# A vision state-space block and a resampled MLP on one core: first loads, filter order, upsampling buffers and downsampling loads rearranged

## The chip, the core and the metric

The program runs on one core of one Trainium2 chip. The core has five instruction streams that run side by side and meet at semaphores: TensorE (PE: matrix products, PEld is its loading of weights), VectorE (DVE), ScalarE (ACT), GpSimd (POOL), and SyncE (SP), which here only issues DMA transfers. Each engine takes its instructions in order, so one that waits holds back everything behind it on its engine. The metric is the device time of one execution in microseconds (us). All data is float32.

## The reference

Eight images of 64 x 64 pixels with 96 channels pass two residual layers. The first is a selective scan over the pixels in four directions (rows and columns, forward and backward); the second is a pointwise quadratic network between an upsampling by two and a low-pass downsampling. Cut to what matters:

```python
# layer 0:  x = x + ss2d(group_norm(x))
xc, z = split(x @ in_proj.T)                       # 192 channels each
xa = silu(depthwise_conv3x3(xc) + conv_b)
xs = stack([xa by rows, xa by columns, both reversed])   # K = 4
dts, B, C = split(x_proj[k] @ xs)
delta = softplus(dt_proj[k] @ dts + dt_b);  A = -exp(A_logs)
h[t] = exp(delta[t] * A) * h[t-1] + delta[t] * xs[t] * B[t]   # 16 states a channel, 4096 steps
y = sum over the four directions of (C . h + D * xs), each turned back
out = (layer_norm(y) * silu(z)) @ out_proj.T
# layer 1:  x = x + mlp(group_norm(x))
h = upsample2_by_fft(x) @ W1.T + b1
h = coef0 + coef1 * h + coef2 * h * h
out = lowpass_by_fft(h @ W2.T + b2)[::2, ::2]
```

## The kernel before

**The scan is the backbone.** An image has 4 directions, 4 chunks of 1024 pixels in each, and 24 tiles in a chunk: a tile is 8 channels x 16 states on 128 partitions and 1024 steps on the free axis. That makes 384 tiles an image and 3072 in all, in the order of the list `tiles`; the direction order is k = 1, 0, 2, 3. For a tile, SP fetches `du` spread over the states (`dub`, L1020), GpSimd multiplies it by B (`bb`, L1026), TensorE spreads delta into PSUM (`pd`, L1032), ScalarE takes its exponential in place (L1039), VectorE runs the recurrence (L1046), and VectorE or, for every third tile, GpSimd multiplies by C (`hc`, L1052). TensorE sums over the states (`py`, L1084), ScalarE copies the sum out (L1117). `hold` keeps the last state for the next chunk (`carry`, L1065). The loop over `i` at the end issues, for each tile, the fetch six tiles ahead, `bb` three ahead and `pd` one ahead.

**All other work is threaded between the tiles.** The order of instructions is written out by hand. Work items are Python generators; each `yield` ends a piece and names what the next piece costs (`pe`, `act`, `dve`, `dma`, and `bank`, one of three PSUM banks). `Side.advance` is called once per tile and issues pieces: first `stores`, then `hurried` (which takes from `urgent`), then `active` (which takes from `queue`), within the budgets of `CAPS`. An item has a greatest number of items that may be active beside it, and a weight; new items start only while the weight begun is below what is due at that tile, and at most two per call. `Side.drain` does the same without budgets until nothing is left; it is used before the loop and after it.

**The items of an image.** `front` loads an image's pixels (`piece`, L500), transposes them into `pad` (L429, copies L433), takes statistics (L435), normalizes (`norm`, L513), and runs twelve filter units (`conv`, L524: nine taps; the filter is the projection times the tap, `w_tap`) and twelve gate units (`gate`, L590). Filter units for the second 64 channels cover two blocks of 512 pixels at once. Results go to DRAM (`u_dram`, L556), and `lay` stores the row order. `prepare` makes a chunk's operands: `begin` loads `u` (L933), `project` makes B and C (`px`, L944, then `br` and `cr`), `delta` makes delta (`pv`, L969) and `du` in thirds (L988, L991). `tail` adds the directions, normalizes, gates and adds the residual into `x1` (L646 to L719). `mlp` upsamples the columns (`up_h`, L768, L769, stored to DRAM by L775), then handles five rows at a time (`rows_`, L804 to L849), then downsamples (`down_h`, load L864, transposes L872, products L878, L882, L892) and stores the image. While image b is scanned, the side work is the `tail` and `mlp` of image b - 1 and the `front` of image b + 1. For the last image `tail` starts in its last direction, and `mlp` is drained after the last scan.

**Before the loop.** The constants come in over SP and ScalarE in turn (`queue`, L154 and following) and are worked up in one block (L218 to L350), on PSUM tiles of their own. Then `front(0)` is drained with its first eight filter units, then the first chunk's `prepare`; then six fetches, and the loop. The second chunk's `begin` is made urgent before the loop, the rest of its `prepare` at i = 0.

**Buffers that matter here.** `up_h` copies two halves of 512 columns into one tile `t1s` of a pair of buffers. `down_h` loads `t3r` into one of two buffers, lets one step pass and then takes a bank; at most two units are between load and end.

Of the kernel before, what the change touches and what calls it, by code (L numbers as in the profile page):

```python
# [8 lines left out]
F32 = mybir.dt.float32  # L9
AF = mybir.ActivationFunctionType  # L10
# [126 lines left out]
def kernel(ctx: ExitStack, tc: tile.TileContext, a: dict, out: bass.AP):  # L137
# [19 lines left out]
    ident = load("ident", [128, 128])  # L157
    grp = load("grp", [C, C])
# [11 lines left out]
    nc.vector.tensor_scalar(cen_w[:, 1, :], mean_w, -1.0, None, ALU.mult)  # L170
    nc.vector.tensor_tensor(cen_w[:, 0, :], ident[:C, :C], mean_w, ALU.subtract)
# [21 lines left out]
    nc.scalar.activation(neg_a, neg_a, AF.Exp)  # L193
    nc.vector.tensor_scalar(neg_a, neg_a, -1.0, None, ALU.mult)
# [22 lines left out]


    pieces = [(0, 0, 64, 0, 0), (1, 0, 32, 0, 64), (1, 32, 64, 1, 0), (2, 0, 64, 1, 32)]
    with tc.tile_pool(name="ps0", bufs=1, space=PSUM) as ps0, tc.tile_pool(name="setup", bufs=1) as c0p:  # L220
        w_cin = load("w_cin", [C, DI], c0p)

        w_tap = convr
        for tap in range(9):
            nc.vector.tensor_tensor(w_tap[:, tap, :], convr[:, tap, :], w_cin, ALU.mult)
        sel_0 = c0p.tile([128, 8, 128], F32, name="sel_0")
        for hf in range(2):
            queue().dma_start(
                sel_0[64 * hf : 64 * hf + 64].rearrange("p j m -> p (j m)"),
                a["sel_b"][0:64, 0:2].rearrange("r q j m -> r (q j m)"),  # L230
            )
        nc.vector.tensor_copy(sel_b, sel_0.rearrange("p j (c n) -> p j n c", n=NS))
        xp_in = [
            c0p.tile([128, K, Q3, R if n == "xp_dt" else NS], F32, name=n) for n in ("xp_dt", "xp_c", "xp_b")
        ]
        d_sum = c0p.tile([128, Q3], F32, name="d_sum")
        ds = c0p.tile([128, Q3, K], F32, name="ds")
        for hf in range(2):
            for q, r0, r1, f, c0 in pieces:
                rows, src = slice(64 * hf + r0, 64 * hf + r1), slice(c0, c0 + r1 - r0)  # L240
                for t, name in zip(xp_in, ("xp_dt", "xp_c", "xp_b")):
                    queue().dma_start(t[rows, :, q, :], a[name][src, :, f, 0 : t.shape[-1]])
                queue().dma_start(ds[rows, q, :], a["ds"][src, f, :])
        nc.gpsimd.memset(xp, 0.0)
        for t, c0 in zip(xp_in, (0, 32, 48)):
            nc.vector.tensor_copy(xp[:, :, :, c0 : c0 + t.shape[-1]], t)
        nc.vector.tensor_reduce(d_sum, ds, mybir.AxisListType.X, ALU.add)
        for q in range(Q3):
            nc.vector.tensor_scalar(d_diag[:, q, :], ident, d_sum[:, q : q + 1], None, ALU.mult)

        ramp = c0p.tile([128, 128], F32, name="ramp")
        ones = c0p.tile([128, 128], F32, name="ones")
        nc.gpsimd.memset(ones, 1.0)
        nc.vector.tensor_tensor_scan(ramp, ones, ones, -1.0, ALU.mult, ALU.add)
        nc.vector.tensor_tensor(ones, ident, ramp, ALU.mult)
        freq = c0p.tile([128, 1], F32, name="freq")
        nc.vector.tensor_reduce(freq, ones, mybir.AxisListType.X, ALU.add)
        NF = 33
        wave = c0p.tile([NF, 2 * (SIDE + 64)], F32, name="wave")
        turn, half, poly = (c0p.tile(wave.shape, F32, name=f"wave{j}") for j in range(3))  # L260
        cols, c0 = {}, 0
        for quarter in range(2):
            for n in (SIDE, 64):
                at = cols[n, quarter] = slice(c0, c0 + n)
                c0 += n
                m, r = wave[:, at], turn[:, at]
                nc.vector.tensor_scalar(m, ramp[:NF, :n], freq[:NF], -quarter * n / 4.0, ALU.mult, ALU.add)

                nc.vector.tensor_scalar(r, m, 1.0 / n, 12582912.0, ALU.mult, ALU.add)
                nc.vector.tensor_scalar(r, r, -12582912.0, -float(n), ALU.add, ALU.mult)  # L270
                nc.vector.tensor_tensor(r, m, r, ALU.add)
                nc.vector.tensor_scalar(half[:, at], r, math.pi / n, None, ALU.mult)
        nc.vector.tensor_tensor(turn, half, half, ALU.mult)
        nc.vector.tensor_scalar(poly, turn, 1.0 / math.factorial(13), -1.0 / math.factorial(11), ALU.mult, ALU.add)
        nc.vector.tensor_tensor(poly, poly, turn, ALU.mult)
        for j in (9, 7, 5, 3):
            c = (1.0 if j % 4 == 1 else -1.0) / math.factorial(j)
            nc.vector.scalar_tensor_tensor(poly, poly, c, turn, ALU.add, ALU.mult)
        nc.vector.scalar_tensor_tensor(poly, poly, 1.0, half, ALU.add, ALU.mult)
        nc.vector.tensor_tensor(poly, poly, poly, ALU.mult)  # L280
        nc.vector.tensor_scalar(wave, poly, -2.0, 1.0, ALU.mult, ALU.add)

        share = c0p.tile([NF, 2], F32, name="share")
        for j, n in enumerate((64, SIDE)):
            nc.vector.tensor_scalar(share[:, j : j + 1], ident[:NF, 0:1], -1.0 / n, 2.0 / n, ALU.mult, ALU.add)
        nc.vector.scalar_tensor_tensor(
            share[:, 1:2], ident[:NF, 32:33], -1.0 / SIDE, share[:, 1:2], ALU.mult, ALU.add
        )
        down_f = c0p.tile([NF, 2, 64], F32, name="down_f")
        up_f = c0p.tile([NF, 2, 2, 64], F32, name="up_f")  # L290
        for quarter in range(2):
            base = wave[:, cols[64, quarter]]
            nc.vector.tensor_scalar(down_f[:, quarter, :], base, share[:, 1:2], None, ALU.mult)
            for j in range(2):
                nc.vector.tensor_scalar(up_f[:, quarter, j, :], base, share[:, 0:1], None, ALU.mult)
        pf = ps0.tile([128, SIDE + 64], F32, name="pf")
        for quarter in range(2):
            grid = wave[:, cols[SIDE, quarter]]
            start, stop = quarter == 0, quarter == 1
            nc.tensor.matmul(  # L300
                pf[:, :SIDE],
                up_f[:, quarter].rearrange("p a j -> p (a j)"),
                grid,
                start=start,
                stop=stop,
                skip_group_check=True,
            )
        for quarter in range(2):
            grid = wave[:, cols[SIDE, quarter]]
            start, stop = quarter == 0, quarter == 1  # L310
            nc.tensor.matmul(
                pf[:SIDE, SIDE:], grid, down_f[:, quarter, :], start=start, stop=stop, skip_group_check=True
            )
# [986 lines left out]
```

## Time and profile before

| | us |
|---|---|
| median of three runs | 11214.56 (11200.23 to 11256.48) |
| the profiled execution | 11227.57 |
| its span, first to last instruction | 11225.8 |
| first filter matmul | 42.97 |
| first scan | 142.55 |
| last scan begins | 10928.46 |

In the profile's lists a row of a timeline has the start, the duration, the engine, the line of the kernel, the operation, the tiles (out<-in), the shapes, the count, and in brackets the idle time of the engine before it and what ended that. A row of the waits has who waited for whom, the total in us, the number of times and the longest. Slices are forty equal parts of the span, each digit the busy tenths. "issue" means that the profile shows nothing that the engine waited for.

### The profile page before, as it was taken

The numbers are of one execution on the slowest core, as the hardware profiler recorded it, in microseconds if no ns is written. First come the engines' busy times: TensorE is split into PE (matmuls) and PEld (weight loads), VectorE is DVE, ScalarE is ACT, GpSimd is POOL, SyncE is SP. The second block draws the span as 40 slices with busy tenths as digits, with TensorE's granted clock in tenths as the row PEclk, the third lists the DMA queues.
The fourth block names the chain that finished last, engine by engine and source line by source line (L and its number), as shares of the span: only waits on it lengthen the run. The fifth ranks groups of instructions, "written<-read, shape, count | busy, mean of one in ns | idle before, by whom it ended". The sixth has DMA issues, their size and how long they took to land. (4 is left out here: it accounts for less than half of the span.)

```text
span 11225.8 us, 137177 instructions
## 1 busy us (share of the span) xinstructions
PE 10052.8 (90%) x45022; PEld 3217.9 (29%) x45022; DVE 10212.6 (91%) x7711; ACT 5906.0 (53%) x8218; POOL 10175.5 (91%) x4665
## 2 busy tenths in 40 slices
PE   7898888999889998899889998899988999889888
PEld 2222222322223222332223322233222332223224
DVE  5999999999999999999999999999999999999980
ACT  4455444656455564555545555455644656455443
POOL 4999999999999999999999999999999999999990
PEclk9999999999999999999999999999999999999998
DMA  5878898899988999888988989889898899988981
GB/s 145 220 201 224 211 232 206 215 225 234 230 206 217 230 231 226 209 221 222 236 213 215 222 215 246 206 216 225 221 240 207 216 225 232 231 208 215 224 198 41
DMA packets 1045102, 2401.26 MB, mean 214 GB/s; under 512 B 293948, under 2 KB 315708, under 8 KB 1044392
## 3 DMA queue, kind: packets, MB, share of 16 engines
q1 hardware_dynamic: 1040872, 2391.03, 85.8%
q8 instruction: 361, 5.91, 0.2%
q14 instruction: 349, 2.86, 0.1%
q10 hardware_dynamic: 3520, 1.46, 0.1%
HBM read 1929.05 MB, written 328.73 MB: 201 GB/s over the span
## 5 line engine op out<-in xcount | busy, mean ns | idle before, releaser
L1026 POOL TENSOR_TENSOR bb<-dub,br 128x1024 f32<-128x1024 f32 x3072 | 7174.5, 2359 | 254.7 <-DMA dub<-du 167.9
L1039 ACT ACTIVATE pd<-pd,neg_a 128x1024 f32<-128x1024 f32 x3072 | 3340.3, 1087 | 4592.7 <-PE pd L1032 4566.6
L1032 PE MATMUL pd<-dl,sel_b 64*128 64x512 f32 x12288 | 3528.3, 647 | 942.1 <-DVE carry L1065 625.6
L1046 DVE TENSOR_TENSOR_SCAN pd<-pd,carry,bb 128x1024 f32<-128x1024 f32 x1536 | 3610.1, 2350 | 287.7 <-ACT carry L1065 117.5
L1052 POOL TENSOR_TENSOR hc<-h,cr 128x1024 f32<-128x1024 f32 x1024 | 2413.9, 2357 | 370.8 <-DVE h L1046 303.1
L1052 DVE TENSOR_TENSOR hc<-pd,cr 128x1024 f32<-128x1024 f32 x2048 | 2508.1, 1225 | 157.2 <-PE py L1084 14.7
L1032 PEld LDWEIGHTS pd<-dl,sel_b 64*128 64x128 f32 x12288 | 967.7, 186 | 3230.9 <-issue 1534.8
L1046 DVE TENSOR_TENSOR_SCAN h<-pd,carry,bb 128x1024 f32<-128x1024 f32 x768 | 1796.2, 2339 | 7.8 <-ACT pd L1039 7.4
L1084 PE MATMUL py<-hc,sel_r 128*32 128x512 f32 x12288 | 1723.2, 620 | 34.6 <-POOL hc L1052 34.4
L1046 DVE TENSOR_TENSOR_SCAN pd<-pd,bb 128x1024 f32<-128x1024 f32 x512 | 1173.1, 2291 | 149.5 <-ACT pd L1039 68.7
L1058 PE MATMUL idle<-sel_b,ident 128*128 128x512 f32 x1654 | 949.4, 656 | 5.2 <-DVE ty L682 5.2
L524 PE MATMUL pc<-pad,convr 96*128 96x512 f32 (+1 forms) x2304 | 858.7, 614 | 2.0 <-issue 2.0
L1046 DVE TENSOR_TENSOR_SCAN h<-pd,bb 128x1024 f32<-128x1024 f32 x256 | 583.3, 2278 | 26.1 <-ACT pd L1039 24.3
L988 POOL TENSOR_TENSOR u<-dl,u 128x512 f32<-128x512 f32 x384 | 486.0, 1272 | 126.9 <-DMA br<-xd 126.7
L1084 PEld LDWEIGHTS py<-hc,sel_r 128*32 128x32 f32 x12288 | 251.1, 109 | 1115.3 <-issue 862.0
L821 PEld LDWEIGHTS p<-w2q,mq 128*100 128x100 f32 x4800 | 452.6, 168 | 274.5 <-issue 214.4
L814 PE MATMUL ph<-xu,w 96*128 96x500 f32 x960 | 505.7, 630 | 11.5 <-ACT mq L815 6.7
L821 PE MATMUL p<-w2q,mq 128*100 128x96 f32 x4800 | 511.1, 258 | 2.3 <-ACT mq L815 2.3
L944 PE MATMUL px<-u,xp 64*64 64x512 f32 x1536 | 427.4, 630 | 37.4 <-DMA u<-u 35.0
L1058 PEld LDWEIGHTS idle<-sel_b,ident 128*128 128x128 f32 x1654 | 252.9, 191 | 613.5 <-issue 575.5
L524 PEld LDWEIGHTS pc<-pad,convr 96*128 96x128 f32 (+1 forms) x2304 | 262.2, 162 | 561.5 <-issue 559.3
L969 PE MATMUL pv<-xd,dt_w 64*64 64x512 f32 x1536 | 398.5, 610 | 2.0 <-ACT xd L954 2.0
(153 smaller groups left out, 6763.1 us busy)
## 6 DMA issues: line engine op xcount, KB each, us to landing
dub<-du SPq DMA_DIRECT2D x3072, 512.0 KB
u<-u SPq DMA_DIRECT2D x256, 384.0 KB
du<-u SPq DMA_DIRECT2D x768, 128.0 KB
y<-yq SPq DMA_DIRECT2D x768, 128.0 KB
br<-xd SPq DMA_DIRECT2D x256, 256.0 KB
cr<-xd SPq DMA_DIRECT2D x256, 256.0 KB
yp<-y SPq DMA_DIRECT2D x384, 128.0 KB
yp<-u SPq DMA_DIRECT2D x192, 128.0 KB
```

The lines of the kernel that those rows point to most:

```text
L524: nc.tensor.matmul(t[rows].rearrange("p (i j) -> p i j", i=8), weights[:, cs], v["pad"][:, 8 * blk + kw : 8 * blk + kw + 8, kh : kh + H], ...
L814: nc.tensor.matmul(t[:, :px], w1[:, m, :], xu, start=True, stop=True)
L821: nc.tensor.matmul(t[:SIDE, C * i : C * i + C], sq[:, m, row], w2q[:, m, :], start=(m == 0), stop=(m == 2))
L944: nc.tensor.matmul(p[rows], xp[rows, k, q, :], v["u"][rows, q, :], start=(q == 0), stop=(q == 2), skip_group_check=True,)
L988: nc.gpsimd.tensor_tensor(v["u"][:, q, :], got["dl"][:, q, :], v["u"][:, q, :], ALU.mult)
L1026: nc.gpsimd.tensor_tensor(t["bb"], t["dub"], t["got"]["br"], ALU.mult)
L1032: nc.tensor.matmul(pd[:, MB * hf : MB * hf + MB], sel_b[rows, 4 * t["s"] + t["j"]].rearrange("p n c -> p (n c)"), t["got"]["dl"][rows, t[" ...
L1039: nc.scalar.activation(pd, pd, AF.Exp, scale=neg_a[:, t["k"], t["g"] : t["g"] + 1])
L1046: nc.vector.tensor_tensor_scan(t["h"][:, ::step], pd[:, ::step], t["bb"][:, ::step], 0.0 if t["first"] else held, ALU.mult, ALU.add)
L1052: (nc.gpsimd if t["by_pool"] else nc.vector).tensor_tensor(t["hc"], t["h"], t["got"]["cr"], ALU.mult)
L1058: nc.tensor.matmul(p, ident, sel_b[:, 0:4].rearrange("p j n c -> p (j n c)"), start=True, stop=True)
L1084: nc.tensor.matmul(py[r0 : r0 + 32], sel_r[:, t["j"], :], t["hc"][:, MB * hf : MB * hf + MB], start=(t["j"] == 0), stop=(t["j"] == 3 and t ...
```

## The change

1. `x1`, the buffer for an image's pixels that `tail` used to take from a pool, becomes a constant tile, and image 0 is loaded into it right behind the first constant, by eight loads on SP. The statistics of image 0 read it in place of loads of their own.
2. The products for `w_tap` move from VectorE to GpSimd. The other small constants are loaded behind the pixels, all over SP (`constants_in`), and are worked up by two items, `constants_of_scans` and `constants_of_mlp`, that are drained together with the first filter units; they take their PSUM from the three side banks.
3. Only four filter units are drained ahead of the first chunk's `prepare`. The next four are the queue while it is issued, with doubled budgets. The second chunk's `begin` is made urgent at i = 2, the rest at i = 4.
4. `up_h` copies each half into a tile of its own, in a ring of five.
5. `down_h` lets four steps pass between the load and the bank. For the last image eight units may be between load and end, with eight buffers in a pool of their own.

```diff
     ident = load("ident", [128, 128])
+    x1 = cp.tile([128, 32, C], F32, name="x1")
+    for w in range(0, 32, 8):
+        for wh in range(2):
+            w0 = 32 * wh + w
+            nc.sync.dma_start(x1[64 * wh : 64 * wh + 64, w : w + 8, :], x[0, :, w0 : w0 + 8, :])
     grp = load("grp", [C, C])
...
+    w_cin = load("w_cin", [C, DI])
+    w_tap = convr
+    for tap in range(9):
+        nc.gpsimd.tensor_tensor(w_tap[:, tap, :], convr[:, tap, :], w_cin, ALU.mult)
...
+    def constants_in():
+        nc.gpsimd.memset(xp, 0.0)
+        raw["sel"] = tile_([128, 8, 128], "sel_0")
...
+                    nc.sync.dma_start(t[rows, :, q, :], a[name][src, :, f, 0 : t.shape[-1]])
+                nc.sync.dma_start(ds[rows, q, :], a["ds"][src, f, :])
...
+    def constants_of_scans():
+        yield {}
+        nc.scalar.activation(neg_a, neg_a, AF.Exp)
+        nc.vector.tensor_scalar(neg_a, neg_a, -1.0, None, ALU.mult)
+        nc.vector.tensor_copy(sel_b, raw["sel"].rearrange("p j (c n) -> p j n c", n=NS))
+        yield dict(bank=1)
+        bank, pt = side.bank("pt")
...
+    def constants_of_mlp():
+        yield {}
+        nc.vector.tensor_scalar(cen_w[:, 1, :], mean_w, -1.0, None, ALU.mult)
...
         def piece(g):
+            if b == 0:
+                return x1[:, 4 * g : 4 * g + 4, :]
             yield dict(dma=200)
...
         if b == 0:
-            return start + convs[:8], convs[8:] + lays + gates + [bp.close()]
+            return start + convs[:4], convs[4:] + lays + gates + [bp.close(), bp.close()]
...
-            keep["x1"] = bp.tile([128, 32, C], F32, tag="x", name="x", bufs=1, depth=0)
+            keep["x1"] = x1
...
+        deep = 8 if b == images - 1 else 2
...
         def up_h(j):
-            s = bp.tile([SIDE, 2, MB], F32, tag="t1s", name="t1s")
+            s = []
...
-                nc.scalar.copy(s[:, wh, :], t[:SIDE])
+                s.append(bp.tile([SIDE, MB], F32, tag="t1s", name="t1s", bufs=5))
+                nc.scalar.copy(s[wh], t[:SIDE])
...
-            while v["rows"] < SIDE // 10 or v.get("down", 0) >= 2:
+            while v["rows"] < SIDE // 10 or v.get("down", 0) >= deep:
                 yield {}
             v["down"] = v.get("down", 0) + 1
-            s = bp.tile([SIDE, 2, 4 * C], F32, tag="t3r", name="t3r", bufs=2, depth=1)
+            s = bp.tile([SIDE, 2, 4 * C], F32, tag="t3r", name="t3r", bufs=deep, depth=1 if deep == 2 else 2)
...
-            yield {}
+            for _ in range(4):
+                yield {}
             yield dict(bank=1, pe=0.95, act=0.8)
...
-            + [bp.close()],
-            [(4, 2, lambda j=j: down_h(j)) for j in range(8)],
-            [bp.close(), bp.close()],
+            + [bp.close()]
+            + [bp.open("deep")] * (deep > 2),
+            [(max(4, deep), 2, lambda j=j: down_h(j)) for j in range(8)],
+            [bp.close()] * (2 + (deep > 2)),
...
-        side.queue, rest = front(0)
+        side.queue = [bp.open("setup")]
+        side.drain()
+        constants_in()
+        start, rest = front(0)
+        side.queue = start[:-4]
+        side.drain()
+        side.queue = start[-4:] + [(8, 0, constants_of_scans), (8, 0, constants_of_mlp)]
         side.drain()
         side.urgent = prepare(0, tiles[0]["k"], tiles[0]["i0"], tiles[0]["got"])
-        side.drain()
+        side.queue, rest = rest[:4], rest[4:]
+        while side.urgent or side.hurried:
+            side.advance({e: (2 * most, 2 * most) for e, (_, most) in Side.CAPS.items()}, 2, 0)
...
-        side.urgent.append(begin)
         total = 1
...
-            if i % NT == 0:
+            if i == 2:
+                side.urgent.append(begin)
+            if i == 4 or i and i % NT == 0:
                 side.urgent += side.later
                 side.later = []
```

## The prediction

> **What bounds the kernel now.** I read the page's busy times and slices first. They say that VectorE and GpSimd are full from slice 1 to slice 38, so a gain has to come from the two ends, or from places inside where both stop.
>
> ```profile
> span 11225.8 us, 137177 instructions
> PE 10052.8 (90%) x45022; PEld 3217.9 (29%) x45022; DVE 10212.6 (91%) x7711; ACT 5906.0 (53%) x8218; POOL 10175.5 (91%) x4665
> DVE  5999999999999999999999999999999999999980
> POOL 4999999999999999999999999999999999999990
> ```
>
> Then the timeline of the first 200 us. The eight filter units take TensorE 64.63 us before any scan. The first scan starts at 142.55, 35 us after they end. The second chunk's projection (L944) is put into TensorE's queue at once and waits there for `u`; all that is behind it waits too, and VectorE loses 14.96 us. The thirteenth scan (tile 12) starts at 199.68.
>
> ```profile
> 42.97 64.63 PE L524 MATMUL pc<-pad,convr 96*128 96x512 f32 x216 [2.00 <-issue]
> 142.55 2.30 DVE L1046 TENSOR_TENSOR_SCAN pd<-pd,bb 128x1024 f32<-128x1024 f32 x1 [10.39 <-POOL bb L1026]
> 155.72 3.75 PE L944 MATMUL px<-u,xp 64*64 64x512 f32 x4 [24.26 <-DMA u<-u]
> 164.66 2.29 DVE L1046 TENSOR_TENSOR_SCAN h<-pd,bb 128x1024 f32<-128x1024 f32 x1 [14.96 <-ACT pd L1039]
> 199.68 2.30 DVE L1046 TENSOR_TENSOR_SCAN pd<-pd,bb 128x1024 f32<-128x1024 f32 x1 [0.31 <-ACT carry L1065]
> ```
>
> Third, the waits inside the loop (200 to 10920 us), and one upsampling and one downsampling stage in the timeline. ScalarE's copy into `t1s` waits for the store that frees its buffer; the exponential behind it is late, and the scan with it. At the end of a downsampling stage TensorE waits for `t3r`.
>
> ```profile
> ACT t1s L769 <- DMA t<-t1s: 88.9, 21, 9.2
> ...
> 3249.08 0.58 ACT L769 COPY t1s<-p 100x512 f32<-100x512 f32 x1 [8.46 <-DMA t<-t1s]
> 3250.75 2.30 DVE L1046 TENSOR_TENSOR_SCAN pd<-pd,bb 128x1024 f32<-128x1024 f32 x1 [7.26 <-ACT pd L1039]
> ...
> 2405.19 1.01 PE L878 MATMUL p<-t3r,down_t 100*64 100x384 f32 x4 [2.29 <-DMA t3r<-t]
> 2413.33 2.36 DVE L1046 TENSOR_TENSOR_SCAN pd<-pd,carry,bb 128x1024 f32<-128x1024 f32 x1 [2.05 <-ACT pd L1039]
> ```
>
> Last, the end: eight downsampling units, one every 6.61 us, each with a wait for `xn`, at half clock (the columns are stretch, TensorE busy, granted clock, DMA share, GB/s).
>
> ```profile
> 11181.05 1.55 PE L878 MATMUL p<-t3r,down_t 100*64 100x384 f32 x4 [0.92 <-ACT xn L874]
> 11187.67 1.55 PE L878 MATMUL p<-t3r,down_t 100*64 100x384 f32 x4 [0.93 <-ACT xn L874]
> ...
> 43.00:47.00 4.00, 4.00 (x5) 0.50 0.02 4
> 47.00:60.00 13.00, 13.00 (x31) 0.99 0.00 0
> 11160.00:11226.00 66.00, 45.01 (x144) 0.53 0.24 65
> ```
>
> **The change, part by part.** The sum is made against the profiled execution (11227.57 us, span 11225.8), which lies 13.0 us above the median of the three runs (11214.56); the difference is then taken off the median.
>
> *Start of the filters (now 42.97).* The pixel loads leave SP's queue at 0.7 instead of 22.7: eight issues of about 0.63 us (twelve took 7.55). They are 1.5 MB; at the 200 GB/s that the loop moves that is 8 us, so they land by about 11. Passed by them on SP: `grp`, two of the `conv_b` loads and six more, 5 us later each. VectorE's queue has the add into `low` (L185) ahead of the statistics; it waits for `conv_b`, at 9.2 now, 12.5 then. Eight statistics steps follow, each a chain transpose 0.61, copies 0.64, statistics 0.69 in two banks: 1.15 each (1.3 now, beside loads), so they end near 21.5. Reduction to `nb` takes 3.2 (38.84 to 42.05) and the first matmul follows 0.9 later: 25.5. Beside it GpSimd makes the nine filters: its 512 and 1024 wide products take 1.27 and 2.36 us, so 192 wide 0.59, nine 5.3; `w_cin` lands near 14, the border memsets follow, 21. Covered, by 4 us; without that cover it delays one for one. All small constants now go over SP, 38 issues at about 0.62, until some 36: covered, since the first store of a filter unit comes at 47 (64.22 now, 21 after the filters' start); were they later, that store would wait 0.62 for each. Bounds for the filters' start: 22 (loads free of each other) and 36 (the copies into `pad` held back by the late border memsets).
>
> The Trainium skill, GPSIMD Engine Reference, § 3.1, speaks against this move: an elementwise product of two tensors costs GpSimd about twice VectorE's time. The rows agree (2.36 against 1.22 for the same product), and by either the nine are off the path.
>
> *Four units ahead of chunk 0.* Now the first four units take 42.97 to 76.4, 33.4; with the new start they end at 58.9. The constants' VectorE chain (13 us of short operations) lies beside units three and four. From the end of the units to `u` in place: 10.7 to 12.4 now (118.35 and 119.96 against 107.6), plus two issues for `dt_w`, 1.5: 72.8. Then TensorE's order decides: all of units five to eight are issued ahead of the first `pd`. 36 filter steps at 0.86 are 31.0; the projection and three `pv` steps, 6 x 0.86, 5.2; `pd` 1.1; the exponential 1.1; 1.7 for the slow clock at the restart: first scan near 113. The data side is ready earlier: last `pv` at 95, its ScalarE, VectorE and GpSimd steps to 100.5, store, load 4.6 and product 2.36: 109. Had the units not been issued there, 109 is what would stand.
>
> *`u` of chunk 1 two tiles later, the projection four.* What was queued behind L944 no longer waits: `u` is issued once the fifth `bb` is done (118) and lands 8 to 10 later (147.75 to 155.7 now), 128; TensorE gets to the projection after tile 3, at 128. So tile 12 comes at 113 + 12 x 3.5 = 155 instead of 199.7: **-44**; I take **-43**. Ends: -20 (start at 36, the wait stays half) and -52.
>
> *Half buffers.* Per stage twelve copies, about two per tile. Today copy 5 waits 4.50 for the first unit's stores and copy 9 8.46 for the third's (issued 3237.84, landed 3249.08, 11.2 behind broadcast loads). With five halves copy 5 finds a free one, and copy 9 takes one stored at 3232. Copy 10 takes copy 5's and must still wait for the store of 3237.84, but one tile later, with one exponential let through. VectorE then loses about 1.6 and 2.7 instead of 1.42 and 7.26: -4.4, seven stages, **-31**. Ends: 0 (the wait only moves) and -66 (all of the 8.7 to 9.8 goes). A loss is excluded: five halves return no later than four.
>
> *Four steps between load and use, images 0 to 6.* The last load of a stage is issued at 2395.7 and used at 2405.2; four tiles are 14 us, so the 2.29 wait, and VectorE's 2.26 and 2.05 behind it, go: -3.5 of 4.3, seven times **-24**, ends 0 and -35. What it adds: two units in flight now pass in seven steps, 28 tiles for eight instead of 26 (L878 runs beside tiles 239 to 265). That is later side work; I charge **+10**, ends 0 and see the third rival.
>
> The first image's pixels stay in `x1` and are loaded into it once more for its residual, as before; the smaller loads of image 0 that this saves stand in the first term. Nothing else in the loop is touched.
>
> *After the last scan.* The upsampling stage (10968 to 10984) has waits of 2.5, 2.2, 1.5 for stores; one half more in flight: **-2** (0 to -5). Downsampling: loads all issued at once; units start in pairs, so that the second transpose covers `xn`. At half clock the starts in one unit are 1.48, 1.66, 0.85 apart, plus 1.06 for the transpose: 5.05 against 6.61, -12. At full clock the same rows are 0.87, 1.13, 0.84 and 0.64 (2310 to 2316), 3.5. The stage was 51; with a first pair at half clock and six at 3.5 it is 29: **-22**. I take that, since the filters' rows above show the clock back after 4 us of unbroken work, and a pair is 8 us of it. Ends -9 (half clock, loads sharing the queue) and -25. The first `t3r` wait (7.53) stays.
>
> The Trainium skill, TensorE: Matmul & The Clock Gate, Part 1, states that the gate opens after about 3.4 us of sustained work and shuts after an idle window as long; its Part 4 adds that transposes do not count as work. By the first the stage is warm, by the second a stage with many transposes might never be: -22 by the one, -12 by the other. The row 43 to 47 agrees with the first; none here shows the second alone.
>
> Sum: -43 - 31 - 24 + 10 - 2 - 22 = -112: 11115.6 for the profiled execution, **11103** for the median.
>
> **Rivals.** *The waits inside only move.* ScalarE still meets the same slow stores, and other waits (GpSimd's 110 for `dub`, 161 us in all) take the place of those removed. Then the loop gives nothing: -43 + 10 - 24 = -57, 11157. For it: the loop has 179 us of scans waiting for ScalarE in 287 places, of which these are few. Against: 5.0 to 8.0 us are lost at the same tile in all seven stages.
>
> *The ends give their lower bounds too.* Filters at 36, down stage cold: -20 - 9 = -29, 11186. For it: the late border memsets; no row shows whether the copies would wait for them.
>
> *Side work slips.* If each of four pairs took three steps more and the pace did not make it up, 12 tiles per image would be carried on: the last gate (L590) starts beside tile 376 of 384, so from a slip of 8 on it decides. Over seven images the last image's blocks (L646 beside tiles 325 to 375) fall behind the last scan, three pairs at the 38 us that the fourth takes there (10930 to 10968): +114, and the down term is lost: -112 + 24 + 114 = +26, 11241. Against: items start by weight, and two may start per tile when behind.
>
> **How the numbers follow.** Forecast 0.60, waits move 0.20, ends low 0.12, slip 0.08. The forecast's own range is 11065 to 11140. Below 11050 and above 11195 I leave out a tenth each: the low side by the bounds of the half buffers and the start, the high side by most of the slip. 0.5% is 56 us, about what a measurement of this kernel can tell from no change (its three runs lie 56 apart). Faster by more than that, below 11158: nearly all of the first case and 0.65 of the second, 0.72; slower, above 11271: half of the slip and what I do not see, 0.07; the rest 0.21.
>
> **What would show it.** First filter matmul near 25.5; first scan near 113 behind `pd`, not behind `bb`; no 15 us wait at tile 2; tile 12 near 155. In each upsampling stage one ScalarE wait for a store, at copy 10, of 4 us. No wait at L878 inside the loop. At the end two transposes in a row, a clock near 1 and a unit every 3.5 us. Wrong if the first filter waits for GpSimd, if the last gate slips past the image's end by more than 8 tiles, or if the loop from tile 12 to the last scan (10729 us now) does not shrink by some 45.

## The result and the profile after

The changed kernel takes **11108.11 us** (median of 4 runs, 11103.48 to 11117.10) against 11221.38 for the kernel before on the same chip (4 runs, 11200.23 to 11256.48): a ratio of **0.9895, 95% interval 0.9883 to 0.9907**. The forecast was 11103, and for the profiled execution 11115.6; the profiled one took 11107.68 (span 11105.8). The size came out well; two of the terms behind it did not, and their errors have opposite signs.

The page of the changed kernel (span, busy times, two rows of slices): VectorE works nearly as long as before (10207.5 us against 10212.6), so all but 5 of the 120 us are idle time that went away.

```profile
span 11105.8 us, 137238 instructions
PE 9967.9 (90%) x45020; PEld 3204.6 (29%) x45020; DVE 10207.5 (92%) x7702; ACT 5910.6 (53%) x8218; POOL 10179.6 (92%) x4674
DVE  6999999999999999999999999999999999999990
POOL 5999999999999999999999999999999999999990
```

I split both executions by the starts of VectorE's scans: up to tile 12, from there to the last scan, and after it; and the loop by chunks of 24 tiles (image, chunk), each from its first scan to the next chunk's. The upsampling stage lies in chunk 4 of an image (tiles 96 to 119), the downsampling stage in chunks 10 and 11 (240 to 287).

| profiled execution, us | before | after | difference | forecast |
|---|---|---|---|---|
| first filter matmul | 42.97 | 23.02 | -20.0 | -17.5 |
| scan of tile 0 | 142.55 | 120.08 | -22.5 | -29.5 |
| start to tile 12 | 199.68 | 164.62 | **-35.1** | -43 |
| tile 12 to the last scan | 10728.8 | 10669.3 | **-59.4** | -45 |
| of it chunk 4, images 1 to 7 | | | -34.7 | -31 |
| of it chunks 10 and 11, images 1 to 7 | | | -25.8 | -24 (+10 elsewhere) |
| last scan to the end | 297.3 | 271.9 | **-25.4** | -24 |

The start, in the timeline of the changed kernel. The filters begin at 23.0. The first scan waits for `pd`, as forecast, but at 120 instead of 113, since `pd` stands behind all of 70.61 to 116.12 in TensorE's queue. The 15 us wait at tile 2 is gone.

```profile
23.02 33.77 PE L562 MATMUL pc<-pad,convr 96*128 96x512 f32 x108 [2.06 <-issue]
69.09 1.59 PE L420 MATMUL pb<-w,sel 128*128 128x96 f32 x6 [1.20 <-DVE sel L416]
70.61 4.10 PE L987 MATMUL px<-u,xp 64*64 64x512 f32 x8
98.82 17.37 PE L562 MATMUL pc<-pad,convr 96*64 96x512 f32 x72 [3.63 <-DVE e L585]
116.12 1.99 PE L1075 MATMUL pd<-dl,sel_b 64*128 64x512 f32 x8
120.08 2.30 DVE L1089 TENSOR_TENSOR_SCAN pd<-pd,bb 128x1024 f32<-128x1024 f32 x1 [8.02 <-ACT pd L1082]
164.62 2.27 DVE L1089 TENSOR_TENSOR_SCAN pd<-pd,bb 128x1024 f32<-128x1024 f32 x1
```

The waits inside the loop of the changed kernel (total, times, longest). Those of ScalarE for stores have halved (88.9 before). TensorE no longer waits for `t3r` there at all, but it waits for something else, the pixels of the next image:

```profile
ACT t1s L810 <- DMA t<-t1s: 43.8, 25, 7.1
PE pt L465 <- DMA x<-in_x: 26.3, 6, 5.7
```

The same view of the kernel before shows both of TensorE's waits, and the second was small:

```profile
PE p L878 <- DMA t3r<-t: 16.2, 6, 3.9
PE pt L429 <- DMA x<-in_x: 8.2, 7, 2.7
```

One of each in the timeline of the changed kernel, third image. At 3202.4 copy 10 of the upsampling stage waits 3.09 us for the store that frees its half, and VectorE loses 1.54 (before, it lost 7.26 behind copy 9). At 3697.0 the transposes of a piece of pixels wait; the sums `py` are queued behind them, and VectorE loses 4.21 at tile 262.

```profile
3202.40 0.59 ACT L810 COPY t1s<-p 100x512 f32<-100x512 f32 x1 [3.09 <-DMA t<-t1s]
3205.02 2.29 DVE L1089 TENSOR_TENSOR_SCAN h<-pd,bb 128x1024 f32<-128x1024 f32 x1 [1.54 <-ACT pd L1082]
...
3697.02 1.06 PE L465 MATMUL pt<-ident,x 128*96 128x128 f32 x4 [5.68 <-DMA x<-in_x]
3699.98 1.23 DVE L1095 TENSOR_TENSOR hc<-pd,cr 128x1024 f32<-128x1024 f32 x1 [4.21 <-PE py L1127]
```

The end: transposes of two units in a row (x8), then units 2.53 us apart within a pair and 6.5 per pair. In the table of stretches (length, TensorE busy, granted clock, DMA share, GB/s) the clock goes from 0.67 to 0.89 (0.50 from 11067 to 11080, 1.00 from 11081 to 11100).

```profile
11069.81 1.55 PE L920 MATMUL p<-t3r,down_t 100*64 100x384 f32 x4 [7.07 <-DMA t3r<-t]
11079.20 1.61 PE L914 MATMUL pn<-ident,x 128*96 128x128 f32 x8
11081.19 0.87 PE L920 MATMUL p<-t3r,down_t 100*64 100x384 f32 x4 [0.37 <-ACT xn L916]
11083.72 0.87 PE L920 MATMUL p<-t3r,down_t 100*64 100x384 f32 x4
11087.68 0.87 PE L920 MATMUL p<-t3r,down_t 100*64 100x384 f32 x4 [0.49 <-ACT xn L916]
...
11060.00:11080.00 20.00, 12.23 (x44) 0.67 0.44 135
11080.00:11106.00 26.00, 17.96 (x106) 0.89 0.25 61
```

### The profile page after: what moved, and what is told of

The parts are those of the page before. It is cut to its first block, busy times and chain, and to the rows that moved or that the text cites. A ratio compares the mean times of both kernels' runs of the same rounds, so it can differ in the third digit from the quotient of the medians.

```text
span 11105.8 us, 137238 instructions
## 1 busy us (share of the span) xinstructions
PE 9967.9 (90%) x45020; PEld 3204.6 (29%) x45020; DVE 10207.5 (92%) x7702; ACT 5910.6 (53%) x8218; POOL 10179.6 (92%) x4674
## 5 line engine op out<-in xcount | busy, mean ns | idle before, releaser
L1069 POOL TENSOR_TENSOR bb<-dub,br 128x1024 f32<-128x1024 f32 x3072 | 7173.5, 2359 | 208.4 <-DMA dub<-du 149.2
L1127 PE MATMUL py<-hc,sel_r 128*32 128x512 f32 x12288 | 1715.0, 617 | 30.4 <-POOL hc L1095 30.2
L562 PEld LDWEIGHTS pc<-pad,convr 96*128 96x128 f32 (+1 forms) x2304 | 266.3, 163 | 563.9 <-issue 552.8
```

Source lines behind the costliest of these rows:

```text
L562: nc.tensor.matmul(t[rows].rearrange("p (i j) -> p i j", i=8), weights[:, cs], v["pad"][:, 8 * blk + kw : 8 * blk + kw + 8, kh : kh + H], ...
L1069: nc.gpsimd.tensor_tensor(t["bb"], t["dub"], t["got"]["br"], ALU.mult)
L1127: nc.tensor.matmul(py[r0 : r0 + 32], sel_r[:, t["j"], :], t["hc"][:, MB * hf : MB * hf + MB], start=(t["j"] == 0), stop=(t["j"] == 3 and t ...
```

## The experiments

All start from the changed kernel. The theory: each part removes a stall at a place of its own, and the parts add up. The rival: waits only move, so the parts overlap or fill each other's place. Times are medians; ratios are to the kernel before, run beside each on its chip (medians 11221.4 to 11227.9; the changed kernel: 0.9895).

| run | us | ratio, 95% interval |
|---|---|---|
| e1 unit buffers | 11153.44 | 0.9936, 0.9924 to 0.9949 |
| e6 four halves | 11135.82 | 0.9927, 0.9913 to 0.9940 |
| e5 twelve halves | 11075.44 | 0.9870, 0.9857 to 0.9884 |
| e2 one step | 11137.45 | 0.9922, 0.9911 to 0.9934 |
| e3 eight units | 11128.29 | 0.9910, 0.9896 to 0.9924 |
| e4 eight units, chunk 1 early | 11140.21 | 0.9920, 0.9906 to 0.9935 |
| e7 two deep in the last image | 11138.85 | 0.9912, 0.9897 to 0.9927 |
| e9 pixels late | 11153.52 | 0.9927, 0.9913 to 0.9941 |
| e10 five steps for the pixels | 11110.57 | 0.9899, 0.9884 to 0.9914 |
| e8 filter products on VectorE | 11104.53 | 0.9893, 0.9878 to 0.9908 |
| b1 twelve halves, new start | 11069.73 | 0.9863, 0.9847 to 0.9880 |
| b2 as b1, five steps | 11076.36 | 0.9869, 0.9855 to 0.9884 |

Executions of one kernel lie up to 56 us apart (before: 11200 to 11256; e1: 11128 to 11177), so I estimate that a median alone is good to some 10 to 20 us; each verdict rests on the place in the trace. There is one trace of each kernel, so a place has its own scatter. The seven kernels whose upsampling stage is that of the changed kernel (e2, e3, e4, e7 to e10) lie 2.9 to 7.0 us above its trace in chunk 4 of images 1 to 7. In chunks 10 and 11, those with its downsampling stage and order of loads (e3, e4, e7, e8, e9) lie between 4.3 below and 1.9 above it.

### The upsampling buffers (e1, e6, e5)

```diff
-                s.append(bp.tile([SIDE, MB], F32, tag="t1s", name="t1s", bufs=5))
-                nc.scalar.copy(s[wh], t[:SIDE])
+                nc.scalar.copy(s[:, wh, :], t[:SIDE])   # s: one tile [SIDE, 2, MB] ahead of the loop, two buffers
```

> The changed kernel with the upsampled rows back in two buffers of a whole unit (two copies each); all else as changed. Theory of separate stalls: copies 5 and 6 of every up stage wait again for the stores of the first unit, VectorE idles 10 to 12 us per image in tiles 110 to 119 instead of 5 to 7.5, and the chunk that holds the up stage gets back what it lost from before to after, 34.7 us over seven images (2.4 us more in the first); the last up stage adds 2. So 1% of nothing else: 11108 + 31 to 39, 11139 to 11147 us. Rival, waits only move (the rest of the change would have taken up the slack without the half buffers): 11108 to 11118 us, and the idle time appears in other tiles instead.

Chunk 4 of images 1 to 7 is 34.1 us longer, the 34.7 of the change back to within 1; that it fits so closely is luck, given the scatter above. The waits for stores (whole span) are 88.0 against 46.6, and they stand at copies 5 and 9 as before (5 and 6 were expected), the long one at 9:

```profile
ACT t1s L809 <- DMA t<-t1s: 88.0, 25, 9.2
...
3213.68 0.59 ACT L809 COPY t1s<-p 100x512 f32<-100x512 f32 x1 [8.06 <-DMA t<-t1s]
3215.36 2.30 DVE L1088 TENSOR_TENSOR_SCAN pd<-pd,bb 128x1024 f32<-128x1024 f32 x1 [6.54 <-ACT pd L1081]
```

The time is 45 us up, 6 more than the expectation allowed; in the profiled execution 10 us of the rest lie in the last image outside the stage and 3.5 after the last scan, while chunks 10 and 11 are 10 shorter.

e6 has `bufs=4` in place of 5:

> The changed kernel with four half buffers instead of five: the bytes of the two unit buffers of before, in halves. If what counts is the fifth buffer (how many copies may run ahead of the first landing), copy 5 overwrites half 0, whose store was issued no earlier than with unit buffers, so the wait is back at copy 5: 11108 + 25 to 37, 11133 to 11145 us, and the ScalarE waits for stores are as long as with unit buffers (near 9 us). If what counts is the granularity (one store of a unit landing frees one copy), most of the gain stays: 11108 to 11118 us.

Chunk 4 is 26.7 longer than with five halves, and the waits are 77.0 against 46.6. The longest wait is 8.9. So the fifth buffer counts: it carries about 27 of the 34. The other 7, for the granularity, are hardly more than the scatter.

e5 has `bufs=12`, which does not fit beside the buffers of the rows stage; the ring gets a pool that is closed first:

```diff
-            [bp.open("rest"), bp.open("mlp"), (1, 1, begin)]
+            [bp.open("rest"), (1, 1, begin), bp.open("up")]
...
-            + [keep["last"], (1, 1, fetch_first)]
+            + [keep["last"], (1, 1, rows_in), bp.close(), bp.open("mlp"), (1, 1, fetch_first)]
```

`rows_in` is the waiting part of `fetch_first`, and `xn` moves into "rest" as before by its new depth.

> The changed kernel with twelve half buffers, one for each copy of an up stage, in a pool of their own that is closed before the rows are fetched. No copy can wait for a store of its own stage. Theory of separate stalls: the wait at copy 10 (3.1 to 7.1 us of ScalarE, 1.5 to 5.4 us of VectorE per image in seven images) goes: 11108 - 17 to 30, 11078 to 11091 us, with VectorE idle in tiles 110 to 119 near 1 to 3 us per image instead of 5 to 7.5. Rival, the wait moves on (the rows can be fetched only when the last store has landed, so the same landing is waited for one stage later): 11103 to 11113 us.

No wait for a store is left in its trace, chunk 4 is 29.9 shorter, and VectorE idles 1.3 to 4.4 us in tiles 110 to 119 of an image instead of 5.6 to 7.6. The theory holds for the stage, at its upper end (the time is 2.6 below its range), and the remaining wait was worth nearly as much as the change's own gain here. Chunks 10 and 11 are 35 shorter too, and the other chunks together give 27 back: the pool's closing shifts the downsampling stage by three or four tiles (247 to 276 instead of 244 to 272), and the wait for pixels does not occur. The run does not separate that shift from the ring.

### The steps between load and use (e2, e10)

```diff
-            for _ in range(4):
-                yield {}
+            yield {}
             yield dict(bank=1, pe=0.95, act=0.8)
```

> The changed kernel with one step instead of four between the load of a down unit and the request for its PSUM bank; eight buffers in the last image stay. Theory of separate stalls: the product of the loaded rows waits again for its load within the loop (16 us of PE waits before), and the columns of the down stage get back what they lost, 25.8 us; in the last image the loads are all issued ahead, so 0 to 3 us there: 11108 + 20 to 29, 11128 to 11137 us. Rival, the load was hidden beside other work anyway: 11103 to 11113 us.

The time is up by 29, as the theory has it, and in the waits within the loop `t3r` is back and the pixels are less. The columns are not as expected: chunks 10 and 11 are 43.9 us longer instead of 25.8, and the other chunks give 14 back (the loop as a whole is 29.8 longer). What gives them back is not shown.

```profile
PE p L919 <- DMA t3r<-t: 23.3, 8, 4.5
PE pt L465 <- DMA x<-in_x: 12.9, 12, 1.8
```

After the last scan nothing changes (272.2), so the steps are a matter of the loop alone. e10 goes after the wait that came in:

```diff
         def piece(g):
...
-            yield {}
-            yield {}
-            yield {}
+            for _ in range(5):
+                yield {}
             return t
```

> The changed kernel with five steps instead of three between the load of a piece of the next image's pixels and its transposes. In the changed kernel TensorE waits 34.9 us in seven places for these pixels (8.7 of it at the start), about one wait of 4 us per image beside the down stage; before, it was 12.3 us in eleven. Theory that this wait took part of the place of the waits for the loaded rows: it goes, and so does what VectorE loses at tile 262 (2.8 us per image): 11108 - 12 to 24, 11084 to 11096 us, with under 12 us of TensorE waits for the pixels. Rival, the wait is filled from elsewhere (the decays run two tiles ahead, or the later pieces move what is behind them): 11103 to 11113 us.

Here the theory fell. The wait is gone (34.9 to 9.3, all of that at the start; first row), and chunk 10 is 23.0 shorter, with VectorE idle 2.5 to 3.7 us in it per image instead of 3.6 to 7.3. But chunk 11 is 22.4 longer, and the time is the same. The next to be late are the broadcast rows `dub`: GpSimd's waits for them rise from 149.2 to 173.2 (in chunk 11 of images 1 to 7 from 9.6 to 30.4), its product `hc` comes late in its queue, TensorE's sums wait for that, and the decay behind the sums is late (fourth image, tile 267).

```profile
PE pt L465 <- DMA x<-in_x: 9.3, 1, 9.3
...
POOL bb L1068 <- DMA dub<-du: 173.2, 132, 5.9
...
5050.43 2.35 POOL L1068 TENSOR_TENSOR bb<-dub,br 128x1024 f32<-128x1024 f32 x1 [2.94 <-DMA dub<-du]
5055.14 1.09 PE L1126 MATMUL py<-hc,sel_r 128*32 128x512 f32 x4 [3.08 <-POOL hc L1094]
5061.15 2.36 DVE L1088 TENSOR_TENSOR_SCAN pd<-pd,carry,bb 128x1024 f32<-128x1024 f32 x1 [5.98 <-ACT pd L1081]
```

So in the upsampling stage waits can be removed one by one, while in the downsampling stage, where loads of `t3r`, pixels, `yp` and `dub` share one queue, this one moved.

### The start (e3, e4, e9, e8)

e3 puts eight units ahead of chunk 0 again:

```diff
-            return start + convs[:4], convs[4:] + lays + gates + [bp.close(), bp.close()]
+            return start + convs[:8], convs[8:] + lays + gates + [bp.close(), bp.close()]
...
-        side.queue, rest = rest[:4], rest[4:]
+        side.queue, rest = rest[:0], rest[0:]
```

> The changed kernel with eight filter units ahead of chunk 0 instead of four (the order of before), pixels first and the later start of chunk 1 kept. Theory that the early pixels and chunk 1's timing carry the start: before, scan 0 came 99.6 us after the first filter matmul with eight units ahead, now 97.1 with four, so four units ahead are worth 2.5 us at scan 0: the other four run beside chunk 0's chain, but all eight still stand ahead of the first decay on TensorE. Scan 0 at 122 to 124 us, tile 12 at 166 to 169, time 11108 + 1 to 5, 11109 to 11113 us. Rival, the four units taken out are the gain: the 33.8 us that four units take on TensorE come back in full or for the most part: scan 0 at 140 to 154 us, time 11128 to 11142 us.

Both theories missed: scan 0 comes at 129.39 (9.3 later), between their ranges, and tile 12 at 174.17 (9.6 later). `pd` is no later than with four units (115.44 against 116.12), since all eight stand ahead of it on TensorE either way. What the four units buy is the data side: `u` of chunk 0 comes 33 us earlier and its products and loads run beside the units. With eight, the first scan waits for `bb` again. (The median is 20 up, at the lower edge of the rival's range; the profiled execution is 10 up, all of it ahead of tile 12.)

```profile
103.56 6.21 PE L987 MATMUL px<-u,xp 64*64 64x512 f32 x12
129.39 2.30 DVE L1089 TENSOR_TENSOR_SCAN pd<-pd,bb 128x1024 f32<-128x1024 f32 x1 [11.27 <-POOL bb L1069]
```

e4 is e3 with chunk 1's preparation started ahead of tile 0 (with four units its data do not exist yet by then):

```diff
+        side.urgent.append(begin)
         total = 1
...
-            if i == 2:
-                side.urgent.append(begin)
-            if i == 4 or i and i % NT == 0:
+            if i % NT == 0:
```

> As the last, and chunk 1's preparation is started ahead of tile 0, as before, instead of at tiles 2 and 4; of the start only the pixels first are left. Theory that chunk 1's timing carries the rest: from scan 0 to tile 12 there were 57.1 us before, with a wait of 15 us at tile 2, and are 44.5 now; the wait comes back: tile 12 at 178 to 183 us, 11 to 15 more than with eight units alone, time 11120 to 11126 us. Rival, the wait at tile 2 came from eight units ahead and not from chunk 1's timing: tile 12 where the kernel with eight units has it or was already 12 us late there, and no difference between the two.

Tile 12 at 185.17, 11.0 later than e3, and the wait at tile 2 is back, behind the projection that waits for `u`. The theory's difference holds; its place was set too early, with e3's miss in it. The median lies 14 above its range; in the profiled execution the loop behind tile 12, in which nothing was changed, is 14.7 longer.

```profile
140.51 3.72 PE L987 MATMUL px<-u,xp 64*64 64x512 f32 x4 [22.52 <-DMA u<-u]
149.48 2.29 DVE L1089 TENSOR_TENSOR_SCAN h<-pd,bb 128x1024 f32<-128x1024 f32 x1 [14.45 <-ACT pd L1082]
```

Against before (199.68) this kernel has the early pixels and what goes with them: 14.5 of the 19.7 that its filters start earlier. So the 35.1 at tile 12, in this order of undoing, are 14.5 for the pixels, 11.0 for chunk 1's timing and 9.6 for the unit order. The 14.5 hold more than the place of eight loads: before, the statistics began at 31.10 without a wait, directly behind the work on the constants in VectorE's queue, and in the changed kernel that work comes after them. No run moves the loads alone.

e9 moves the eight pixel loads behind all constants:

```diff
-    for w in range(0, 32, 8): ...   # the loads of x1
...
         constants_in()
+        for w in range(0, 32, 8): ...
```

> The changed kernel with the first image's pixels loaded behind all constants on SyncE's queue; nothing else moved. The constants take 29.6 us to issue from 12.73 to 42.3 and stand ahead of the pixels then, so the first filter matmul goes from 23.0 to 52 to 54 us. Theory that the start is one serial chain from the pixels to scan 0: scan 0 from 120.1 to 148 to 151 us, and the time 11108 + 27 to 31, 11135 to 11139 us. Rival, something else than the pixels is late as well (the constants of the scans, the weights), so part of the delay is hidden: scan 0 at 125 to 145 us, 11113 to 11130 us.

First filter matmul at 50.56 (+27.5, a little short of the range), scan 0 at 147.94 (+27.9), tile 12 at 190.93 (+26.3): the start is one serial chain. The median rose by 45, though; 20 of it are in the profiled execution's loop, spread over chunks in which nothing was changed and the last image. I take that for the scatter of the loop, which a second trace would have to show; the expectation for the time, which had none, was too narrow.

e8 puts the nine filter products back on VectorE:

```diff
-        nc.gpsimd.tensor_tensor(w_tap[:, tap, :], convr[:, tap, :], w_cin, ALU.mult)
+        nc.vector.tensor_tensor(w_tap[:, tap, :], convr[:, tap, :], w_cin, ALU.mult)
```

> The changed kernel with the nine products of filter taps and input weights on VectorE, ahead of the statistics in its queue, instead of on GpSimd. On GpSimd they start at 14.43 us, when the weights have landed, and end at 19.4, beside the statistics that VectorE makes from 12.35 to 19.0. Theory that VectorE's order counts: the products hold the statistics until 14.4 plus nine times 0.25 to 0.3 us, so these end near 22 us, the first filter matmul comes at 25 to 28 us instead of 23.0, scan 0 as much later, and 11108 + 2 to 5, 11110 to 11113 us. Rival, it makes no difference where they are: first filter matmul at 23 to 24 us, 11103 to 11113 us.

```profile
14.66 2.50 DVE L224 TENSOR_TENSOR convr<-convr,w_cin 96x192 f32<-96x192 f32 x9 [0.56 <-DMA w_cin<-in_w_cin]
26.05 34.02 PE L562 MATMUL pc<-pad,convr 96*128 96x512 f32 x108 [2.07 <-issue]
```

The nine cost 2.50 us on VectorE against 4.96 on GpSimd, but they stand among the statistics, and the filters start 2 to 3 later (23.0 to 24.1 in the kernels whose start was not changed), as the theory has it. The slower engine was the right one, for its queue was empty. Neither scan 0 (123.15; 120.1 to 123.4 in the others) nor the time (11104.53) shows it; 2 to 3 us are below what they can tell.

### After the last scan (e7)

```diff
-        deep = 8 if b == images - 1 else 2
+        deep = 2
```

> The changed kernel with two buffers for the loaded rows in the last image too, as in the others; the four steps stay. Theory that the buffers of the last image are the gain after the last scan: the loop is as it is (within 3 us), and from the last scan to the end it takes 288 to 296 us instead of 271.9; the down units come one by one again, each after its load, with TensorE's granted clock near half: 11124 to 11132 us. Rival, the four steps or the up stage made the gain there: 271 to 276 us after the last scan, 11106 to 11112 us.

289.0 us after the last scan against 271.9, the loop unchanged (10670.5): the place is as the theory has it, the size at its lower edge. Units come one by one, 6.61 us each, for six units at half clock (stretches as above):

```profile
11077.67 1.55 PE L920 MATMUL p<-t3r,down_t 100*64 100x384 f32 x4 [0.86 <-ACT xn L916]
11084.28 1.55 PE L920 MATMUL p<-t3r,down_t 100*64 100x384 f32 x4 [0.93 <-ACT xn L916]
11114.53 0.87 PE L920 MATMUL p<-t3r,down_t 100*64 100x384 f32 x4 [0.93 <-ACT xn L916]
...
11070.00:11108.00 38.00, 32.32 (x103) 0.50 0.26 72
11108.00:11123.00 15.00, 7.28 (x38) 0.84 0.26 69
```

The clock opened for the last two, which it did not before; that makes this stage 5 us shorter than before's and the difference smaller than expected. The median lies 7 above the expectation, the profiled execution (11125.5) inside it.

### A better version (b1, b2)

b1 joins e5's ring with another order of the start:

```diff
+        first = prepare(0, tiles[0]["k"], tiles[0]["i0"], tiles[0]["got"])
+        side.urgent, side.queue = first[:1], rest[:2]
+        side.drain()
+        side.urgent, early = first[1:], False
         while side.urgent or side.hurried:
+            side.advance(None, 2, 0)
+            if not early and "ready" in tiles[0]["got"]: ...   # fetch tiles 0 to 5, product 0, decay 0
...
+        decay(tiles[1])
+        side.queue, rest = rest[2:4], rest[4:]
```

> The changed kernel with twelve half buffers (11075 us by itself) and a reordered start: chunk 0's data are loaded after four filter units, units five and six stand ahead of the projections on TensorE (it idled 13.8 us there), the rows of tiles 0 to 5 are fetched as soon as the first third is ready, tiles 0 and 1 have their decays ahead of units seven and eight, chunk 1 starts at tiles 4 and 6. Theory that the start is one serial chain: scan 0 at 94 to 104 us instead of 121, tile 12 16 to 26 us earlier, 11075 - 16 to 26, 11049 to 11059 us. Rival, units seven and eight or chunk 1's data are late next: tile 12 less than 10 us earlier, 11065 to 11080 us.

Scan 0 comes at 113.6, not at 94 to 104, and tile 12 at 158.5, 5.9 earlier than in e5: the rival's range. The theory's mistake is plain in the trace: TensorE's idle time after the fourth unit is not a wait for `u` alone, the MLP's constants stand in its queue there. Units five and six start at 71.60, behind the same `pb` that ends there, and push the projection to 90.04.

```profile
70.22 1.59 PE L420 MATMUL pb<-w,sel 128*128 128x96 f32 x6 [1.20 <-DVE sel L416]
71.60 18.51 PE L562 MATMUL pc<-pad,convr 96*128 96x512 f32 x36
90.04 2.79 PE L990 MATMUL px<-u,xp 64*64 64x512 f32 x12
```

b2 adds e10's five steps:

> As the last, with five steps instead of three between the load of a piece of pixels and its transposes too. With twelve half buffers TensorE waited for these pixels only at the start (9.3 us in one wait), so the longer lead has no wait to remove: 0 to -5 us against the last kernel, 11044 to 11060 us. Rival, two more steps per piece push the work of the next image back: 5 to 15 us slower than the last.

It is 7 us slower than b1 in the median, within the rival's 5 to 15, with intervals that overlap. Neither differs from e5 by its interval. b1 (0.9863, 0.9847 to 0.9880) is the one whose interval lies below the changed kernel's: 38 us less by medians, nearly all of it the ring's.

## Why the prediction was right, point by point

**Start: forecast -43, measured -35.1.** The mechanism held (filters early, first scan behind `pd`, no wait at tile 2). The failing step is the stretch on TensorE from the projection to `pd`: forecast 36 filter steps at 0.86 (31.0), six projection steps (5.2) and 1.7 for the clock, 37.9; measured 45.5, from 70.61 to 116.12. The filter steps took 34.2 (0.95 each), the projection and `pv` 8.2, and a wait for a side bank that VectorE frees behind ScalarE (`e`, L585) 3.6, which the forecast had nowhere. Then ScalarE has the last unit's activations (116.24 to 119.0) ahead of the first exponential, so from `pd` to scan 0 it takes 4.0 instead of 2.2. The earlier start takes 2.2 off, and scan 0 comes 7 later than forecast; that is 7 of the 9.6 us by which tile 12 misses 155. The projection's start was nearly met (70.6 against 72.8), in part by luck: it stood behind the MLP's constants (`pb`, to 70.7), which the forecast did not have there, and the load of `u` moved its last bytes at 70.2, so both were about equally late.

Within the first 23 us two errors cancelled. The eight pixel loads left SP's queue in 11.9 us, not 5: six of them at 0.63 each, as forecast, the last two only from 8.85 on (rows below). But the add into `low` did not stand ahead of the statistics, which began at 12.35 and ended at 19.0 (21.5 forecast). The nine products cost 0.55 each (0.59 forecast) and end at 19.4, before the filters need them, so "covered" held; the border memsets did not follow them but ran ahead, at 2.2. e8 shows the other side, 2 to 3 us on VectorE. The Trainium skill (GPSIMD Engine Reference, § 3.1) has GpSimd at about twice VectorE's time for an elementwise operation on two tensors (its figures are for an add); 4.96 against 2.50 agrees, and the order in the queue outweighs it.

```profile
0.74 3.78 SPq L163 DMA_DIRECT2D x<-in_x  x6
8.85 3.83 SPq L163 DMA_DIRECT2D x<-in_x  x2
```

**Half buffers: forecast -31, measured -34.7**, undone +34.1 (-27.7 to -31.8 by the traces of the seven other kernels with this stage). Copy 5 goes free and copy 10 waits 3.0 to 7.1 us, as written; copies 6, 7, 11 and 12 wait up to 1.3 now and then. The upper end, -66, is also real: e5 takes away the wait that is left, for 29.9 more.

**Four steps: forecast -24 and +10, measured -25.8 and nothing.** The waits for `t3r` in the loop went from 16.2 us to none. The +10 was the wrong give-back. The side queue did get later, by the 7 tiles that the third rival needed 8 of (the last gate starts beside tile 382 instead of 375, and at 375 again in e2), and cost nothing that can be seen. What came in instead is a wait that the prediction did not name, TensorE's for the next image's pixels, 8.2 to 26.3 us; it is inside the -25.8. So the term is mis-sized as such: 10 charged, nothing found, and with the 4 and 2 us that the other two terms gained, that is the loop's error.

**After the last scan: forecast -2 and -22, measured -3.6 and -21.9** (last scan to the first `t3r` unit 239.4 and 235.8; from there to the end 57.9 and 36.0). The second pair of units has the full clock. The first pair has 9.4 us of products without a gap and without a transpose (11069.8 to 11079.2), and the clock is up 1.2 us later; so the rule of Part 1 in the Trainium skill (TensorE: Matmul & The Clock Gate), a few us of sustained work, fits, but this stage cannot tell it from Part 4, that transposes do not count as work. The start of b1 can: TensorE had run nothing but twelve transposes, 2.77 us of them, when the next twelve took 1.84. The trace's clock goes up at 12.5, between the two. There the transposes counted, against Part 4.

```profile
9.44 2.77 PE L465 MATMUL pt<-ident,x 128*96 128x128 f32 x12 [9.44 <-DMA x<-in_x]
13.85 1.84 PE L465 MATMUL pt<-ident,x 128*96 128x128 f32 x12 [1.65 <-DVE st L471]
```

The forecast's cold case (-12) was misread, which touches only its low bound: it took the steps within a unit at half clock as 1.48, 1.66 and 0.85, and the unit at 11181 of the kernel before has 1.48, 1.82 and 1.33, which makes it about -7.

**Rivals.** "Waits only move" does not hold for the upsampling stage (e1, e5) and does for what is left in the downsampling stage (e10). "Ends low" fell with the filters at 23.0. "Side work slips" stopped one tile short of the point that the prediction gave.

The forecast for the whole was closer than its parts: the start missed by +8, the loop by -14, the end by -1.4; that the first two nearly cancel is luck.

## What to carry to other kernels

Split two traces by a regular event of the bound engine (here each scan): a difference of 1% then falls into a few places, and each part of a change can be charged on its own, to some 5 us here, even where medians scatter by 20 us. A ring's length is set by how many writes may run ahead of the first landing: four to five halves gave 27 us, five to twelve 30 more, the granularity 7 at most. Before a wait on a shared queue is removed, look for what is next in that queue; and before idle time of an engine is filled, look for the instruction that stands first in its queue, not for the data that come later.

## What the runs showed of the hardware that was not expected

- TensorE's clock stayed at half through units of 5.7 us of unbroken work with gaps of 0.9 us (e7: 0.50 over 38 us, TensorE 85% busy; before: eight units, 0.50 over 51 us). In the changed kernel it went up at 11080.4, behind two units that followed each other without a gap. The Trainium skill (TensorE: Matmul & The Clock Gate, Part 1) describes a free-running window of about 3.4 us. In the clock records of all fourteen traces every change is a whole multiple of 3.41 us after the one before it, which agrees. What a window needs is open: in e7 the one from 11085.44 to 11088.85 was busy throughout and the clock stayed at 0.50, and in b1 2.77 us of transposes were enough.
- Eight DMA issues for 1.5 MB of pixels held SP's queue for 11.94 us at the start of the program: six left at 0.63 each, then the queue stood 4.3 us before the seventh and 2.9 before the eighth. The small constants behind them left it at about 0.6 each.
- The loop's length differs by up to some 20 us between traces of kernels whose loop has the same code (e9: 10689.6 against 10669.3), while the start (scan 0 at 120.1 to 123.4) and the end (270.9 to 273.1, though 266.3 in b2) repeat more closely where their code is the same.
